# Step sizes as sixteen output rows, B.C as two half-array products, and a new order of the queues in a two-direction state-space kernel

## The chip, the core and the metric

The kernel runs on one core of a Trainium2 chip. The time is the device time of one execution in microseconds (us); lower is better. A core has engines that each work through their own queue in order: TensorE (PE) for matmuls, VectorE (DVE), ScalarE (ACT), GpSimd (POOL), and SyncE (SP), which here only issues transfers (DMAs). TensorE writes its results to PSUM[...]; everything else lies in SBUF, with 128 partitions (rows). An engine waits for another where it needs that one's result, or where a buffer that it is to fill is still being read.

## What is computed

For 8 sequences of 512 tokens with 256 features, a layer norm is followed by two state-space blocks (one forward in time, one on the reversed sequence), whose outputs are projected, joined and added to the input; then a second layer norm and a linear map with a low-rank part are added.

```python
def _mamba2(x, Win, convw, convb, dtb, Alog, Dsk, normw, Wout):
    zxbcdt = x @ Win
    z, xBC, dt = jnp.split(zxbcdt, [D_INNER, D_INNER + CONV_CH], axis=-1)
    xBC = jax.lax.conv_general_dilated(xBC, convw, window_strides=(1,), padding=[(D_CONV - 1, 0)], dimension_numbers=('NLC', 'LIO', 'NLC'), feature_group_count=CONV_CH) + convb
    xBC = _silu(xBC)
    xs, Bm, Cm = jnp.split(xBC, [D_INNER, D_INNER + NGROUPS * D_STATE], axis=-1)
    dt = jax.nn.softplus(dt + dtb)
    A = -jnp.exp(Alog)
    dA = jnp.exp(dt * A)

    def step(h, inp):
        dA_t, dt_t, B_t, C_t, x_t = inp
        dBx = jnp.einsum('bh,bn,bhp->bhpn', dt_t, B_t, x_t)
        h = dA_t[:, :, None, None] * h + dBx
        y = jnp.einsum('bn,bhpn->bhp', C_t, h)
        return (h, y)
...
    y = jnp.transpose(ys, (1, 0, 2, 3)) + Dsk[None, None, :, None] * xs
    y = y.reshape(b, l, D_INNER)
    y = y * _silu(z)
    y = y * jax.lax.rsqrt(jnp.mean(y * y, axis=-1, keepdims=True) + 1e-05) * normw
    return y @ Wout
```

There are 8 heads of 64 values, the state has 64 rows, and the convolution has 4 taps per channel. The step sizes `dt` are eight numbers for each token and direction. They decide how fast the state decays, so they are needed before anything else of a chunk can be worked out.

## The kernel before

**Tiling.** A sequence is cut into 4 chunks of 128 tokens. A chunk is computed in closed form: decays between each two tokens of the chunk (`lam`) times the products of C and B between them (`cb`), times x; and the state `h` that comes in from the chunk before. The unit of work is a `Pair` (sequence b, chunk c): the forward direction on chunk c and the backward one on chunk 3 - c. The main loop (L817) makes one pass, a *round*, for each of the 32 pairs. In round i the pair `p` is finished, the next one, `q`, is prepared, blocks of a later sequence are projected and convolved (`work`, from the table `todo`, L792), and the `Tail` of an older chunk (output projection, residual, second norm, last linear map) is carried on. Sequences are taken two by two for the step sizes (`Steps`).

**The order is written by hand.** `pin()` (L60) makes each engine run its instructions in the order in which the program text issues them. So moving a line in the loop moves every instruction that it issues within its engine's queue.

**The parts that matter here, with their lines:**
- `steps_v` (L267): projects the step sizes of two sequences. The weights `wdt` (L103) are 8 columns in a field of zeros; a shifted window of 128 columns puts the 8 heads of each chunk, sequence and direction at their own 8 rows of one 128 x 128 result `pdt`. That takes 16 matmuls (an fp32 matmul makes two records in the profile). ScalarE then computes v, |v| and exp(-|v|) (L281 to L283); `ratio` and `series` (L296, L304) finish softplus on VectorE.
- `Block` (L366): `project` (L372, PE, `pp`), `tap` (L389, ACT), `convolve` (L392, three VectorE operations that read `pp` from PSUM), `silu` (L412). The block `NBLK` holds B and C of one direction; its `silu` writes three tiles of 64 rows each: `bb`, `cbd` (C set into a tile that is zero elsewhere, so that one matmul gives both directions side by side) and `cc`.
- `Pair`: `fetch` (L456, transfers of the decay factors into `lam`), `scan` (L483, DVE), `turn` (L492, PE transposes and ACT copies to `xs`), `scale_x` (L500, POOL), `cb` (L511, PE), `mix` (L519, DVE: lam times cb), `skip` (L524, ACT), `gate` (L532, PE) and `gate_silu` (L544, ACT), `scale_c` (L476, POOL, tile `dec`), `decay_state` (L549, POOL), `outputs` (L557, PE, `py`), `add_state` (L577: a PE product `pst`, then an ACT copy in chunk 0 or a DVE add), `evict` (L591, DVE), `times_gate` (L595, POOL), `square` (L599), `norm_sum`, `norm_mean`, `norm_power` (L602 to L611), `presum` (L616, POOL).
- `Tail`: `bias1` (L632, POOL), `project` (L635, PE, `pm`), `residual` (L645, DVE, with the statistics of the second norm), `scales` (L652, POOL), `norm2` (L655, ACT), `bias2` (L667, POOL), `turn` (L670), `ffn` (L677, `pf`), `add_ffn` (L682, DVE), `store` (L685).
- `turn1` (L251): transposes of a later sequence's normed input (`pxh`), in chunks 1 and 3 of even sequences. `prepare_wf` (L207): weights of the last map, once, in round 2.
- PSUM: one bank for the seed, three for `p_proj`, two for `p_tr` (small products and transposes, `cb` among them) and two for `p_y`. The banks of a pool are handed out in turn, and a new tile waits until its bank's last reader is done.

Of the kernel before, what the change touches and what calls it, by code (L numbers as in the profile page):

```python
# [8 lines left out]
F32 = mybir.dt.float32  # L9
AF = mybir.ActivationFunctionType  # L10
ALU = mybir.AluOpType
# [3 lines left out]
P = 128  # L15
NB, L, DM = 8, 512, 256
# [15 lines left out]
def tile_bimamba_ffn(  # L32
# [55 lines left out]
    def ps(p, shape, name):  # L88
        return p.tile(shape, F32, name=name, tag=p.name)
# [23 lines left out]
    def load_win(d, cols):  # L113
        sp.dma_start(out=win_sb[:, d, :, cols], in_=win[d].rearrange("(k p) n -> p k n", p=P)[:, :, cols])
# [8 lines left out]
    for d in range(2):  # L123
        act.dma_start(
            out=wdt[:, :, 56 + 64 * d:64 + 64 * d],
            in_=win[d].rearrange("(k p) n -> p k n", p=P)[:, :, DT0:DT0 + NH],
        )
        rows = slice(d * 64, (d + 1) * 64)
        for to, j in ((dtb_col, 0), (a_col, 1)):
            act.dma_start(  # L130
                out=to[rows, :], in_=heads[j, d].unsqueeze(0).unsqueeze(2).to_broadcast([NC * NSG, NH, 1])
            )
    for d in range(2):
        load_win(d, slice(0, XBC0))
    for d in range(2):
        sp.dma_start(out=normw_sb[:, d], in_=normw[d].rearrange("(k p) -> p k", p=P))
        for two in range(2):
            sp.dma_start(
                out=dcol[two * HD:(two + 1) * HD, d, :],
                in_=heads[2, d].rearrange("(k two) -> two k", two=2)[two:two + 1, :].to_broadcast([HD, NBLK]),  # L140
            )
# [22 lines left out]
    pool.memset(samed[64:, 64:], 1.0)  # L164
    fold = const.tile([P, 64], F32, name="fold")
    pool.tensor_tensor(fold, ident[:, :64], ident[:, 64:], ALU.add)

    cbd = []
    for i in range(2):
        cbd.append(const.tile([P, NC, 2, P], F32, name=f"cbd{i}"))  # L170
        pool.memset(cbd[i], 0.0)

    wy = const.tile([P, 2, NBLK, DM], F32, name="wy")
    wf = const.tile([P, NK, DM], F32, name="wf")
# [87 lines left out]
    def sm(name, b0, shape=(P, P), bufs=1):  # L262
        return small.tile(list(shape), F32, name=f"{name}_{b0}", tag=name, bufs=bufs)

    F, W = slice(0, 64), slice(64, P)

    def steps_v(b0):  # L267

        pd = ps(p_tr, [P, P], f"pdt_{b0}")
        n = 0  # L270
        for i in range(NSG):
            for c in range(NC):
                w0 = 56 - (c * NSG + i) * NH
                for k in range(NK):
                    pe.matmul(  # L275
                        pd, lhsT=wdt[:, k, w0:w0 + P], rhs=seq[b0 + i]["xhT"][:, k, c * P:(c + 1) * P],
                        start=(n == 0), stop=(n == NSG * NC * NK - 1),
                    )
                    n += 1
        v, e = sm("v", b0), sm("e", b0)  # L280
        act.activation(v, pd, AF.Identity, bias=dtb_col[:, 0:1])  # L281
        act.activation(e, v, AF.Abs)
        act.activation(e, e, AF.Exp, scale=-1.0)  # L283
        return v, e

    class Steps:

# [78 lines left out]
    class Block:  # L366
# [45 lines left out]
        def silu(self):  # L412
            b, d, s = self.b, self.d, self.s
            if self.blk < NBLK:
                act.activation(self.acc, self.acc, AF.Silu)  # L415
                return
            if "bb" not in s:
                s["bb"] = seqp.tile([P, NC, P], F32, name=f"bb_{b}", tag="bb")
                s["cc"] = seqp.tile([P, NC, P], F32, name=f"cc_{b}", tag="cc")
            bs, cs = slice(0, NS), slice(NS, P)  # L420
            for to, rows in ((s["bb"], bs), (cbd[b % 2][:, :, d, :], cs), (s["cc"], cs)):
                half = to[d * NS:(d + 1) * NS]
                act.activation(
                    half if d == 0 else half[:, ::-1, :],
                    self.acc[rows, :].rearrange("p (c t) -> p c t", c=NC), AF.Silu,
                )
# [12 lines left out]
    class Pair:  # L439
# [70 lines left out]

        def cb(m):  # L511

            m.pcb = ps(p_tr, [P, 2, P], f"cb_{m.name}")
            pe.matmul(
                m.pcb.rearrange("p d t -> p (d t)"), lhsT=m.s["bb"][:, m.c, :],
                rhs=cbd[m.b % 2][:, m.c].rearrange("p d t -> p (d t)"), start=True, stop=True,
            )

        def mix(m, d):  # L519
            dve.tensor_tensor(  # L520
                m.lam[d], m.lam[d], m.pcb[:, d, :].unsqueeze(1).to_broadcast([P, NH, P]), ALU.mult
            )

        def skip(m, d):  # L524
# [52 lines left out]
        def add_state(m):  # L577
            if m.c == NC - 1:
                return
            pst = ps(p_proj, [P, DI], f"pst_{m.name}")  # L580
            for d in range(2):
                rows = slice(d * NS, (d + 1) * NS)
                pe.matmul(pst[rows, :], lhsT=m.s["bn"][:, m.c, rows], rhs=m.xw[d], start=True, stop=True)  # L583
            if m.c == 0:
                m.h_new = m.tile("h", (P, DI))
                act.copy(m.h_new, pst)
            else:
                dve.tensor_tensor(m.h_new, m.h_new, pst, ALU.add)
            m.s["h"] = m.h_new

        def evict(m, d):  # L591
# [221 lines left out]
    def begun(at):  # L813
        return [tails[j] for j in range(n) if begin[j] == at]

    st = late = before = None
    for i in range(n):  # L817
        p, q = pairs[i], pairs.get(i + 1)
        b, c = order[i]
# [9 lines left out]
                pairs[i + 2].fetch()  # L829
        if (c == 0 if even else c == 1) and b + 3 < NB:  # L830
            load(b + 3)
        when(t0, "scales", "norm2", "bias2")
        p.decay_state()
        p.outputs()
        for d in range(2):
# [1 line left out]
            p.times_gate(d)  # L837
        p.add_state()
        when(before, "norm_sum", "norm_mean")
        if q:  # L840
            for d in range(2):
                q.turn(d)
        when(work[0], "project", "tap")
        when(t0, "turn")
        for d in range(2):
# [4 lines left out]
        if st and not even and c == 2:  # L850
            st.exponential()
        if q:
            q.cb()
            q.gate(0)
            q.gate_silu(0)
            for d in range(2):
                q.scale_x(d)
            q.scan(0)
        if q:
            q.scan(1)  # L860
# [7 lines left out]
        if st and not even and c == 2:  # L868
# [2 lines left out]
            pairs[i + 2] = Pair(*order[i + 2])  # L871
            pairs[i + 2].fetch()
        when(t0, "ffn", "add_ffn")
        when(before, "norm_power")
        if q:
            q.scale_c()
        when(t, "bias1")
        p.presum()
        if st and not even and c == 2:
            st.weigh()  # L880
# [12 lines left out]
        when(work[1], "project", "tap")  # L893
        if i < 2:
            prepare_wy(i, range(2, NBLK))
        if q:
            q.skip(1)
        when(work[1], "convolve")
        if i == 2:
            prepare_wf()  # L900
        if i == 0:
            steps_last(0)
            steps_total(0)
        if not even and c == 3 and ahead < NB:
            steps_total(ahead)
        if st and not even and c == 1:
            st.ratio()
            st.series()
        if q:
# [2 lines left out]
        if even and c in (1, 3) and ahead < NB:  # L912
            turn1(ahead + (c == 3), 0)
            turn1(ahead + (c == 3), 1)
        if c == 2 and b + 1 < NB:
            tokenwise_b(b + 1)
        when(work[1], "silu")
# [74 lines left out]
```

## Time and profile before

| | |
|---|---|
| Three runs | 665.66 us median, 665.1 to 667.6 |
| The profiled execution | 668.52 us, span from first to last instruction 666.5 us |
| Mean granted TensorE clock | 0.983 of full speed |
| Step-size projection `pdt`, L275 | 128 records in four calls, 15.0 us busy |
| B.C `cb`, L514 | 64 records, 20.1 us busy |
| `cbd` activations, L423 | 16, 10.1 us busy |
| First bias add, L633, and second, L668 (POOL) | 32 each, 23.3 us busy each |
| Table loads of ScalarE | 12 in the loop, 1.28 us each, and those of the start |

The profiled execution took 2.0 us more than its span, and 2.9 us more than the median of the three runs. Busy time of a group is time in which at least one of its instructions ran. A line of the timeline has start and length in us, engine, line, operation, output and inputs, shapes, and in brackets the idle time of the engine before it with the instruction that ended it. TensorE is busy for 94% of the span; but a share of busy time is an average over stretches that are limited by different engines, and matmuls are pipelined, so that the lines of the rounds have to be read one by one.

### The profile page before, as it was taken

How to read it: one execution, taken by the hardware profiler on the slowest of the kernel's cores; microseconds unless marked ns; L12 is line 12 of the kernel's file. 1: busy time of each engine (PE TensorE's matmuls, PEld its weight loads, DVE VectorE, ACT ScalarE, POOL GpSimd, SP SyncE). 2: the span in 40 equal slices, each digit the busy share in tenths (PEclk: the TensorE clock that was granted, in tenths of full speed). 3: DMA queues.
4: the chain of work that ended last, by engine and by line, in shares of the span. 5: the costliest groups of instructions: out<-in, count | busy, mean ns of one | idle time of the engine just before them, and what ended most of it. 6: DMA issues, size and time to landing. Idle time of an engine off the chain costs nothing.

```text
span 666.5 us, 12446 instructions
## 1 busy us (share of the span) xinstructions
PE 623.3 (94%) x4652; PEld 478.5 (72%) x4652; DVE 542.0 (81%) x827; ACT 399.8 (60%) x855; POOL 467.2 (70%) x572
## 2 busy tenths in 40 slices
PE   4968998999999999999999999999999998999996
PEld 2556676777776777877777677777877777787785
DVE  4788888788988899977988998877998887886643
ACT  2787565876566565875476574686576654564421
POOL 4447455677854888757856789638876679599983
PEclk9979998999999999999999998999999998999998
DMA  7555332313055312134045322332005432333010
GB/s 207 161 168 143 111 104 49 86 42 102 18 182 142 112 62 90 59 92 143 17 135 147 92 64 80 112 112 103 25 13 179 104 111 80 111 112 111 17 49 32
DMA packets 34940, 64.63 MB, mean 97 GB/s; under 512 B 7680, under 2 KB 22080, under 8 KB 34880
## 3 DMA queue, kind: packets, MB, share of 16 engines
q1 hardware_dynamic: 32736, 63.79, 31.8%
q8 instruction: 37, 0.61, 0.4%
q10 hardware_dynamic: 2144, 0.04, 0.2%
q14 instruction: 23, 0.19, 0.1%
HBM read 59.10 MB, written 4.72 MB: 96 GB/s over the span
## 4 chain that ended last, share of the span: by engine, by line
PE 51%; DVE 24%; POOL 13%; ACT 7%; issue 4%; DVEq 0%; POOLq 0%; ACTq 0%
PE pm L640 11%; PE pp L379 9%; PE pz L538 9%; PE py L563 9%; DVE xc L397 7%; DVE lam L490 4%; PE pf L680 3%; POOL yg L597 3%; DVE lam L520 3%; PE pxs L496 3%; POOL xdt L507 2%; PE pdt L275 2%; DVE x L647 2%; ACT xc L390 2%; PE pst L583 2%
## 5 line engine op out<-in xcount | busy, mean ns | idle before, releaser
L397 DVE SCALAR_TENSOR_TENSOR xc<-pp,conv_sb,xc 128x511 f32<-128x511 f32 x183 | 136.0, 744 | 46.3 <-ACT xc L390 41.9
L379 PE MATMUL pp<-xhT,win_sb 128*128 128x512 f32 x320 | 151.2, 600 | 0.5 <-ACT xhT L710 0.5
L490 DVE TENSOR_TENSOR_SCAN lam<-lam,seed 128x512 f32<-128x512 f32 x128 | 145.6, 1200 | 0.0
L538 PEld LDWEIGHTS pz<-xhT,win_sb 128*128 128x128 f32 x1024 | 125.7, 194 | 10.3 <-issue 7.7
L538 PE MATMUL pz<-xhT,win_sb 128*128 128x128 f32 x1024 | 126.6, 277 | 0.0
L640 PE MATMUL pm<-wy,yg 128*128 128x256 f32 x512 | 115.5, 379 | 0.0
L640 PEld LDWEIGHTS pm<-wy,yg 128*128 128x128 f32 x512 | 97.1, 190 | 13.1
L379 PEld LDWEIGHTS pp<-xhT,win_sb 128*128 128x128 f32 x320 | 57.8, 194 | 45.7 <-issue 42.6
L528 ACT ACTIVATE yg<-xc,dcol 128x128 f32<-128x128 f32 x256 | 80.9, 393 | 0.0
L390 ACT ACTIVATE xc<-pp,conv_sb 128x512 f32<-128x512 f32 x64 | 49.3, 774 | 44.9 <-PE pp L379 44.7
L520 DVE TENSOR_TENSOR lam<-lam,cb 128x1024 f32<-128x1024 f32 x64 | 75.0, 1212 | 0.1
L668 POOL TENSOR_TENSOR x<-x,bf_sb 128x256 f32<-128x256 f32 x32 | 23.3, 729 | 73.6 <-ACT xh L657 71.5
L507 POOL TENSOR_TENSOR xdt<-xs,dw 128x512 f32<-128x512 f32 x64 | 66.5, 1046 | 6.6 <-ACT xs L498 6.6
L563 PE MATMUL py<-lam,xdt 128*64 128x128 f32 x1024 | 66.3, 285 | 0.0
L415 ACT ACTIVATE xc<-xc 128x512 f32<-128x512 f32 x64 | 39.5, 628 | 43.7 <-DVE xc L397 43.4
L563 PEld LDWEIGHTS py<-lam,xdt 128*64 128x64 f32 x1024 | 58.6, 143 | 7.5 <-issue 4.6
L593 DVE TENSOR_TENSOR yg<-py,yg 128x512 f32<-128x512 f32 x64 | 42.2, 685 | 18.0 <-PE py L563 15.5
L507 POOL TENSOR_TENSOR xs<-xs,dw 128x512 f32<-128x512 f32 x48 | 50.1, 1045 | 3.8
L647 DVE SCALAR_TENSOR_TENSOR x<-pm,rms,x 128x256 f32<-128x256 f32 x64 | 30.9, 483 | 25.4 <-POOL x L633 16.5
L496 PE MATMUL pxs<-ident,xc 128*128 128x128 f32 x256 | 39.7, 286 | 12.5 <-ACT rms L609 5.1
L498 ACT COPY xs<-pxs 128x512 f32<-128x512 f32 x64 | 36.1, 586 | 15.4 <-PE pxs L496 15.2
L496 PEld LDWEIGHTS pxs<-ident,xc 128*128 128x128 f32 x256 | 29.8, 151 | 19.2 <-ACT rms L609 6.8
(445 smaller groups left out, 996.0 us busy)
## 6 DMA issues: line engine op xcount, KB each, us to landing
lam<-dat SPq DMA_DIRECT2D x64, 512.0 KB, 5.2
x<-in_x_dram SPq DMA_DIRECT2D x36, 128.0 KB, 2.2
out_dram<-x SPq DMA_DIRECT2D x32, 128.0 KB, 1.7
x<-in_x_dram SPq DMA_DIRECT2D x7, 512.0 KB, 6.8
win_sb<-in_win_dram SPq DMA_DIRECT2D x2, 640.0 KB, 5.8
win_sb<-in_win_dram SPq DMA_DIRECT2D x2, 512.0 KB, 7.9
wot<-in_wout_t_dram SPq DMA_DIRECT2D x2, 512.0 KB, 12.4
wo_sb<-in_wo_dram SPq DMA_DIRECT2D x2, 256.0 KB, 8.9
```

The source lines that it names most:

```text
L379: pe.matmul(pp, lhsT=win_sb[:, d, k, c0:c0 + P], rhs=s["xhT"][:, k, :], start=(k == 0), stop=(k == NK - 1),)
L390: act.activation(self.acc, self.pp, AF.Identity, bias=self.w[:, 4:5], scale=self.w[:, 3:4])
L397: dve.scalar_tensor_tensor(self.acc[:, to], self.pp[:, of], self.w[:, 3 - j:4 - j], self.acc[:, to], ALU.mult, ALU.add,)
L490: dve.tensor_tensor_scan(lam, lam, sd, 0.0, ALU.mult, ALU.add)
L496: pe.transpose(pt[:, blk * P:(blk + 1) * P], m.s["xc", d][:, blk, m.tcol[d]], ident)
L507: pool.tensor_tensor(hb(to), hb(m.xw[d]), dw[:, j, cols].unsqueeze(2).to_broadcast([P, NH, HD]), ALU.mult)
L520: dve.tensor_tensor(m.lam[d], m.lam[d], m.pcb[:, d, :].unsqueeze(1).to_broadcast([P, NH, P]), ALU.mult)
L528: act.activation(yg[:, blk, :], m.s["xc", d][:, blk, m.tcol[d]], AF.Copy, scale=dcol[:, d, blk:blk + 1])
L538: pe.matmul(pz[:, blk, :], lhsT=win_sb[:, d, k, blk * P:(blk + 1) * P], rhs=m.s["xhT"][:, k, m.tcol[d]], start=(k == 0), stop=(k == NK - 1),)
L563: pe.matmul(m.py[d][two * HD:(two + 1) * HD, blk, :], lhsT=lhsT, rhs=rhs, start=first, stop=last, skip_group_check=True,)
L640: pe.matmul(t.pm[:, d, :], lhsT=yg[:, blk, :], rhs=wy[:, d, blk, :], start=(blk == 0), stop=(blk == NBLK - 1),)
L647: dve.scalar_tensor_tensor(t.x1[:, 0, :], t.pm[:, d, :], t.s["rs", d, t.c], t.x1[:, 0, :], ALU.mult, ALU.add)
```

## The change

For sequences 2 to 7 (two at a time, three calls), `steps_raw` replaces `steps_v`: the weights `wd2` hold the 16 columns of both directions; each sequence's 512 tokens stream once for each half of the features, and the 16 rows of result for the first sequence go to rows 0 to 15, those of the second to rows 64 to 79 of one PSUM tile. ScalarE copies them out, and 16 small transfers move each group of 8 rows x 128 tokens to the rows at which `Steps` wants them. The softplus operations of ScalarE move from the end of chunk 3 of an even sequence to chunk 1 of the following one. Sequences 0 and 1 still use `steps_v`.

B.C becomes two matmuls, one per direction, that contract 64 rows each (rows 0 to 63 and 64 to 127) and write two PSUM tiles; `cbd` and its activation go. The rest are moves in the loop.

```diff
+    wd2 = const.tile([P, NK, 2 * NH], F32, name="wd2")
     for d in range(2):
         load_win(d, slice(0, XBC0))
+        sp.dma_start(
+            out=wd2[:, :, d * NH:(d + 1) * NH],
+            in_=win[d].rearrange("(k p) n -> p k n", p=P)[:, :, DT0:DT0 + NH],
+        )
...
-    cbd = []
-    for i in range(2):
-        cbd.append(const.tile([P, NC, 2, P], F32, name=f"cbd{i}"))
-        pool.memset(cbd[i], 0.0)
...
+    def softplus_v(b0, of):
+        v, e = sm("v", b0), sm("e", b0)
+        act.activation(v, of, AF.Identity, bias=dtb_col[:, 0:1])
+        act.activation(e, v, AF.Abs)
+        act.activation(e, e, AF.Exp, scale=-1.0)
+        return v, e
+
+    def steps_raw(b0):
+
+        pd = ps(p_tr, [P, L], f"pdt_{b0}")
+        for k in range(NK):
+            for i in range(NSG):
+                pe.matmul(
+                    pd[64 * i:64 * i + 2 * NH, :], lhsT=wd2[:, k, :], rhs=seq[b0 + i]["xhT"][:, k, :],
+                    start=(k == 0), stop=(k == NK - 1), skip_group_check=True,
+                )
+        raw = convp.tile([P, L], F32, name=f"raw_{b0}", tag="raw", bufs=1)
+        for i in range(NSG):
+            rows = slice(64 * i, 64 * i + 2 * NH)
+            act.copy(raw[rows, :], pd[rows, :])
+        rows = sm("rows", b0)
+        for d in range(2):
+            for c in range(NC):
+                for i in range(NSG):
+                    r = d * 64 + (c * NSG + i) * NH
+                    sp.dma_start(
+                        out=rows[r:r + NH, :], in_=raw[64 * i + d * NH:64 * i + (d + 1) * NH, c * P:(c + 1) * P]
+                    )
+        return rows
...
-            for to, rows in ((s["bb"], bs), (cbd[b % 2][:, :, d, :], cs), (s["cc"], cs)):
+            for to, rows in ((s["bb"], bs), (s["cc"], cs)):
...
-            m.pcb = ps(p_tr, [P, 2, P], f"cb_{m.name}")
-            pe.matmul(
-                m.pcb.rearrange("p d t -> p (d t)"), lhsT=m.s["bb"][:, m.c, :],
-                rhs=cbd[m.b % 2][:, m.c].rearrange("p d t -> p (d t)"), start=True, stop=True,
-            )
+            m.pcb = [ps(p_tr, [P, P], f"cb_{m.name}_{d}") for d in range(2)]
+            for d in range(2):
+                rows = slice(d * NS, (d + 1) * NS)
+                pe.matmul(
+                    m.pcb[d], lhsT=m.s["bb"][rows, m.c, :], rhs=m.s["cc"][rows, m.c, :], start=True, stop=True
+                )
...
-        when(t0, "scales", "norm2", "bias2")
+        when(t0, "scales")
+        if work[0] is None:
+            when(t0, "norm2", "bias2")
         p.decay_state()
         p.outputs()
...
         p.add_state()
         when(before, "norm_sum", "norm_mean")
+        p.new_state()
         if q:
             for d in range(2):
                 q.turn(d)
+        if work[0] is not None:
+            when(t0, "norm2")
         when(work[0], "project", "tap")
...
         if q:
+            q.gate(0)
             q.cb()
-            q.gate(0)
             q.gate_silu(0)
             for d in range(2):
                 q.scale_x(d)
+        if work[0] is not None:
+            when(t0, "bias2")
+        if q:
             q.scan(0)
...
         when(t0, "ffn", "add_ffn")
+        when(t, "bias1")
         when(before, "norm_power")
         if q:
             q.scale_c()
-        when(t, "bias1")
         p.presum()
...
-        if q:
-            q.skip(1)
+        elif i == 2:
+            prepare_wf()
         when(work[1], "convolve")
-        if i == 2:
-            prepare_wf()
...
-        if st and not even and c == 1:
+        if raw is not None and c == 1:
+            st = Steps(b + 1, *softplus_v(b + 1, raw))
+            raw = None
             st.ratio()
             st.series()
...
+        if q:
+            q.skip(1)
         if c == 2 and b + 1 < NB:
             tokenwise_b(b + 1)
...
         if even and c == 3 and ahead < NB:
-            st = Steps(ahead, *steps_v(ahead))
+            raw = steps_raw(ahead)
```

`new_state` is the second half of the old `add_state` (the copy or the add that makes the new `h`), now behind `norm_sum` and `norm_mean`. `norm2` and `bias2` keep their old place only in the last five rounds, in which no later sequence is projected (`work[0]` is None).

More of the change, by code (lines that the diff above doesn't have):

```diff
@@ L279, in steps_v @@
                     n += 1
[L280 to L284, printed above, removed]
+        return softplus_v(b0, pd)
     class Steps:
@@ L511, in cb @@
         def cb(m):
-            m.pcb = ps(p_tr, [P, 2, P], f"cb_{m.name}")
-            pe.matmul(
-                m.pcb.rearrange("p d t -> p (d t)"), lhsT=m.s["bb"][:, m.c, :],
-                rhs=cbd[m.b % 2][:, m.c].rearrange("p d t -> p (d t)"), start=True, stop=True,
-            )
+            m.pcb = [ps(p_tr, [P, P], f"cb_{m.name}_{d}") for d in range(2)]
[4 more added lines that the diff above has]
+                )
         def mix(m, d):
             dve.tensor_tensor(
-                m.lam[d], m.lam[d], m.pcb[:, d, :].unsqueeze(1).to_broadcast([P, NH, P]), ALU.mult
+                m.lam[d], m.lam[d], m.pcb[d].unsqueeze(1).to_broadcast([P, NH, P]), ALU.mult
             )
@@ L579, in add_state @@
                 return
-            pst = ps(p_proj, [P, DI], f"pst_{m.name}")
+            pst = m.pst = ps(p_proj, [P, DI], f"pst_{m.name}")
             for d in range(2):
@@ L583, in add_state, with new_state @@
                 pe.matmul(pst[rows, :], lhsT=m.s["bn"][:, m.c, rows], rhs=m.xw[d], start=True, stop=True)
+        def new_state(m):
+            if m.c == NC - 1:
+                return
             if m.c == 0:
                 m.h_new = m.tile("h", (P, DI))
-                act.copy(m.h_new, pst)
+                act.copy(m.h_new, m.pst)
             else:
-                dve.tensor_tensor(m.h_new, m.h_new, pst, ALU.add)
+                dve.tensor_tensor(m.h_new, m.h_new, m.pst, ALU.add)
             m.s["h"] = m.h_new
@@ L814, in begun @@
         return [tails[j] for j in range(n) if begin[j] == at]
-    st = late = before = None
+    st = raw = late = before = None
     for i in range(n):
```

## The prediction

> **What bounds the kernel now.** I read the busy line of the page first, then the busy time round by round, then the table of waits, then the timeline of the rounds in which a wait ends last. A "round" is one pass of the main loop (one chunk of one sequence); I number them 0 to 31 and take the first state product `py` (L563) as a round's start.
>
> ```profile
> PE 623.3 (94%) x4652; PEld 478.5 (72%) x4652; DVE 542.0 (81%) x827; ACT 399.8 (60%) x855; POOL 467.2 (70%) x572
> ```
>
> TensorE (PE) looks like the bound. Rounds 10 to 15 say more (eight rounds, two sequences, make one period of the same work) (columns: stretch, length, then PE, PEld, DVE, ACT, POOL busy, clock, DMA share, GB/s):
>
> ```profile
> 246.00:266.10 20.10, 19.72 (x152) 14.66 (x151) 17.72 (x32) 9.82 (x22) 16.14 (x20) 1.00 0.33 117
> 266.10:288.70 22.60, 22.60 (x185) 18.56 (x184) 17.83 (x25) 17.05 (x35) 13.30 (x20) 1.00 0.40 117
> 288.70:306.70 18.00, 18.00 (x117) 13.32 (x116) 15.30 (x21) 13.20 (x27) 14.12 (x16) 1.00 0.26 77
> 306.70:322.30 15.60, 15.60 (x141) 12.82 (x140) 13.88 (x19) 9.21 (x21) 12.66 (x12) 1.00 0.22 69
> 322.30:343.50 21.20, 20.35 (x157) 15.07 (x157) 20.31 (x42) 13.14 (x27) 15.96 (x21) 1.00 0.07 20
> 343.50:362.90 19.40, 18.59 (x147) 14.16 (x146) 17.59 (x27) 12.58 (x29) 12.54 (x18) 1.00 0.60 189
> ```
>
> Rounds 11 to 13 leave TensorE no gap; in round 14 VectorE (DVE) is busy 20.31 of 21.20 us and TensorE waits for it. So the bound changes hands: TensorE to about 307 us, VectorE after it. The waits say what holds VectorE up:
>
> ```profile
> DVE xc L397 <- ACT xc L390: 41.9, 24, 3.0
> DVE x L647 <- POOL x L633: 16.5, 10, 3.9
> ```
>
> The first is largely a loop of its own: VectorE ends one convolution, ScalarE (ACT) does that block's silu and only then the next block's first tap (0.63 + 0.76 us), and VectorE waits 1.43 us. No faster TensorE shortens that. The second is the bias add L633, queued on GpSimd (POOL) behind `dec` (L479). The turn of rounds 11 and 12 shows both kinds:
>
> ```profile
> 285.07 3.73 PE L275 MATMUL pdt<-xhT,wdt 128*128 128x128 f32 x32
> 285.55 0.63 ACT L423 ACTIVATE cbd<-acc 64x512 f32<-64x512 f32 x1
> 287.53 2.32 DVE L397 SCALAR_TENSOR_TENSOR xc<-pp,conv_sb,xc 128x511 f32<-128x511 f32 x3 [3.00 <-ACT xc L390]
> ...
> 302.91 1.00 DVE L647 SCALAR_TENSOR_TENSOR x<-pm,rms,x 128x256 f32<-128x256 f32 x2 [2.21 <-POOL x L633]
> 303.34 0.78 ACT L390 ACTIVATE xc<-pp,conv_sb 128x512 f32<-128x512 f32 x1 [2.26 <-PE pp L379]
> 304.51 2.28 DVE L397 SCALAR_TENSOR_TENSOR xc<-pp,conv_sb,xc 128x511 f32<-128x511 f32 x3
> ```
>
> And round 13 shows what a matmul costs, by the distance from one group's start to the next:
>
> ```profile
> 306.74 1.10 PE L563 MATMUL py<-dec__2751,h__2819 64*64 64x128 f32 x32
> 307.77 1.97 PE L563 MATMUL py<-lam,xdt 128*64 128x128 f32 x32
> 309.57 1.03 PE L583 MATMUL pst<-xs,bn 128*64 128x512 f32 x4
> 310.52 0.61 PE L605 MATMUL ss<-ones,sz__2645 128*128 128x1 f32 x4
> 313.91 0.60 PE L514 MATMUL cb<-cbd,bb 128*128 128x256 f32 x2
> 314.35 1.95 PE L538 MATMUL pz<-xhT,win_sb 128*128 128x128 f32 x16
> ```
>
> A record (half of an fp32 matmul) of 256 columns takes (314.35-313.91)/2 = 0.22 us, so 128 columns take 0.11 and 512 take 0.43. `pst` has four of 512 in 0.95 us, not 1.7: its two column groups overlap. The 32 records of the first `py` line take 1.03 us, not 3.5: four tiles overlap. Overlapped streaming alone would be 32/4 x 0.11 = 0.88 there and 0.86 for `pst`; the rest, 0.09 to 0.15 us, is paid where the shape of the tiles changes.
>
> [...]
>
> **The change part by part.**
>
> *Step sizes.* `steps_v` took 3.67 us of TensorE (285.07 to 288.74). `steps_raw` has 4 matmuls, 8 records of 512 columns in two column groups: 4 x 0.43 = 1.72 us[...]: 1.9. Saved: 1.75 us, three times (rounds 3, 11, 19). Two ScalarE copies (0.59 each, from L498) replace the three activations and a table load there (2.3 us); those move to chunk 1 of the next sequence, where they run while VectorE still has mixing and residual to do: exp ends some 1.5 us before `ratio` wants it; uncovered, that would be 2.3 us. SyncE issues 16 small transfers more (0.44 us each, as one of the pair `lam<-dat` that takes 0.88: 7 us), queued before the next `lam` and `dec` fetches. Those were issued at 281.69 and 282.66 and slip to about 296; `lam` lands 5.2 us later (page, median), and its scan starts at 312.25. Two rounds lie between the transfers and `ratio`, so I cost them at nothing. The two transfers of `wd2` at the start go before weights that are first used some 30 us later.
>
> *B.C in row groups.* Stream: 4 records of 128 overlapping in twos, 0.22 us[...]: 0.40 to 0.52, where it took 0.44. I take +0.06 a round, +0.2 by the tap of round 12; ends -0.2 (changes free) and +0.3. So this part gains nothing on TensorE. It takes away an activation of 0.63 us (`cbd`) per block. At the end of an even sequence's chunk 3 the moved `skip(1)` (4 x 0.3 us) stands before the same activations and eats that; at the end of an odd one nothing does. Two PSUM buffers are now held until both `mix` are through; the transpose `pxh`, which already waited 1.11 us for the last `mix`, waits for the same end. B.C itself now waits for the copies of both transposes before it, with `pf` and `pm` queued behind; in round 12 those copies end at 295.91 (xT, L675), and the new place, behind a gate projection of 1.78 us, is 296.7.
>
> *The bias adds, `norm2`, `new_state`, `prepare_wf`.* GpSimd adds the first bias ahead of `dec` (2.36 us earlier), so the 16.5 us of waits shrink to those for `norm_power`. `norm2` behind the copies of x is covered by the projection (1.72 us against 1.7 for copies and norm). `dec` ends up to 1.4 us later; in rounds 10 and 18 it is then just in time for `py`.
>
> **The sum for a period.** Rounds 11 to 13: VectorE could come 2.2 us sooner (wait of 302.91), but the convolution of 304.51 needs a tap that TensorE releases: 1.75 - 0.2 sooner, plus the 0.39 us that the tap was early (304.12 to 304.51): 1.9. Rounds 13 to 18 are VectorE and its ScalarE loop; there 0.6 (`cbd` at 364.72) and 0.7 (the bias wait at 380.18) go. Together 3.2 us.
>
> Rounds 2 to 9: TensorE waits 2.41 us before the `py` at 110.95 for `wf`, which VectorE now does 2.2 us sooner. VectorE gains only 0.3 by this (the 1.43 us loop stands free again), then about 1.1 at round 3's end (0.5 before the convolution of 127.64, the rest at 132.86), 2.2 at the bias wait of 146.35, 0.6 and 0.7 as above: 4.9. Rounds 10 to 17 and 18 to 25: 3.2 each. Prologue 0.6 (one `cbd` on the chain at 36.46; the zeroing of `cbd` at 3.1 us is covered, ScalarE's table load ends only at 8.71). Round 0: 0.6. From round 27 GpSimd is busy without a stop but for 0.7 us a round, and its work is the same: 0.8 for rounds 26 to 31. Sum: 0.6 + 0.6 + 4.9 + 3.2 + 3.2 + 0.8 = 13.3 us. The profiled execution took 668.52 us (span 666.5 and 2.0 around it), which gives 655.2; it was 2.9 above the median of the runs shown, so for the median 652.4: I say 652.
>
> **The rivals.**
> 1. *The 16-wide column groups don't overlap* (the part does not do what it says). Then `steps_raw` is 8 x 0.43 = 3.4[...], as before, and round 12 gains 0.2 in place of 1.9: two periods of 1.5, sum 9.9, 656. For it: no 16-wide tile is in the trace. Against: `pst` overlaps at 64.
> 2. *VectorE's waits all go* and TensorE never holds it: 2.2 + 0.6 + 0.6 + 0.7 + 1.0 (the wait of 1.16 for `h` in round 10) = 5.1 a period, and the half-speed `py` stretches at 401 and 555 us (3.2 us together) don't return: sum 0.6 + 0.6 + 4.9 + 10.2 + 3.2 + 0.8 = 20.3, 645. Against: the tap of 303.34 waits for TensorE.
> 3. *Slower[...].* In place of 0.44 us it would take 0.43 of serial stream[...]: 1.3, or 0.9 x 32 = 28.8 us more on TensorE. Less the 13.3, and some 5 that TensorE's present gaps take up: about 676. It decides from 0.85 us per B.C on (13.3/32 more). For it: no 64-row, 128-column tile is in the trace.[...]
> 4. *No change*: `skip(1)`, the later `dec` and the held PSUM buffers together give back some 0.36 us a round (11.5 in all): 664. For it: `skip(1)` eats one `cbd` already; against: the others have the slack named above.
>
> **How the numbers follow.** Chances: my forecast 0.52, rival 1 0.17, rival 2 0.11, rival 3 0.13, rival 4 0.07. My forecast's own range is 647 to 658 (B.C's two ends, +-0.3 x 16 rounds in which TensorE leads, about 5). With rivals 1, 2 and part of 4 the range is 642 to 663. About 0.5% (3.3 us) is what can be told from no change. Faster by more: 0.52 + 0.17 + 0.11 = 0.80; within: 0.07; slower: 0.13.
>
> **What would show it.** Right: `pd` at about 1.9 us; B.C at 0.4 to 0.5; residual L647's wait for GpSimd near 2 or 3 us in all; convolution waits of 2.72 near 2.1 and of 3.00 hardly less; `py` of round 3 without its 2.41. Wrong: B.C over 0.8; a new wait of `evict` for `skip(1)`, or of `ratio` for the exp; `py` waiting for `dec`; TensorE without gaps in rounds 14 to 16.

## The result, and the profile after

The changed kernel takes 655.27 us (median of 4 runs, 654.47 to 656.33); beside it the kernel before took 665.38 (662.96 to 667.6). The ratio is 0.9852, with a 95% interval of 0.9823 to 0.9881: 10.1 us less. The profiled executions are further apart, 668.52 before and 655.07 after; point 1 on the prediction says what is known of that.

In the changed kernel the state product `py` is at L591, the gate projection `pz` at L566, B.C at L543, the step sizes at L280, the convolution at L424 and its first tap at L417, the residual at L679, the two bias adds at L665 and L700, `dec` at L506. First the busy line of the page of the changed kernel:

```profile
PE 616.7 (94%) x4644; PEld 464.5 (71%) x4644; DVE 541.6 (83%) x827; ACT 393.8 (60%) x845; POOL 463.8 (71%) x570
```

TensorE is busy for 6.6 us less, and its share of the shorter span is the same 94%. The stretches of rounds 10 to 15 (same columns as before, cut at the starts of `py`):

```profile
240.40:260.10 19.70, 19.69 (x157) 14.65 (x157) 17.52 (x31) 10.33 (x26) 17.00 (x23) 1.00 0.41 134
260.10:281.11 21.01, 21.01 (x163) 15.12 (x162) 16.29 (x22) 15.59 (x34) 12.59 (x18) 1.00 0.13 39
281.11:299.29 18.18, 18.18 (x120) 13.31 (x118) 16.37 (x22) 11.02 (x25) 14.01 (x16) 1.00 0.29 86
299.29:315.07 15.78, 15.78 (x144) 12.82 (x143) 14.20 (x19) 10.90 (x23) 12.30 (x13) 1.00 0.58 161
315.07:335.90 20.83, 20.07 (x157) 14.87 (x156) 20.01 (x40) 14.67 (x32) 16.04 (x21) 1.00 0.07 19
335.90:355.74 19.84, 18.80 (x149) 14.18 (x148) 17.92 (x28) 12.10 (x29) 12.71 (x18) 1.00 0.61 187
```

Rounds 10 to 13 now have no gap on TensorE at all, so their lengths are simply the sum of what TensorE does. Round 11 lost 1.56 us (22.62 before, 21.06 now). Rounds 12 and 13 became longer by 0.18 each, which is the new B.C; in round 11, 1.75 us saved on the step sizes less the same 0.18 make the 1.56. Rounds 14 and 15 are still VectorE's; round 15 grew by 0.4. Two waits of the changed kernel answer to the two shown of before:

```profile
DVE xc L424 <- ACT xc L417: 45.6, 27, 3.5
DVE x L679 <- POOL x L665: 1.9, 1, 1.9
```

The bias wait fell from 16.5 to 1.9 us; one other wait of the residual for GpSimd, 3.0 us in round 31, is new. The convolution's wait rose from 41.9 to 45.6. The turn of rounds 11 and 12 shows where it rose (timeline of the changed kernel; VectorE, ScalarE and TensorE):

```profile
281.65 2.31 DVE L424 SCALAR_TENSOR_TENSOR xc<-pp,conv_sb,xc 128x511 f32<-128x511 f32 x3 [3.50 <-ACT xc L417]
...
278.23 1.29 ACT L556 ACTIVATE yg<-xc,dcol 128x128 f32<-128x128 f32 x4
279.55 0.63 ACT L450 ACTIVATE bb<-acc 64x512 f32<-64x512 f32 x1
...
279.29 1.90 PE L280 MATMUL pdt<-xhT,wd 128*16 128x512 f32 x8
```

The moved `skip(1)` (L556) stands in ScalarE's queue ahead of the silus of B and C and of the next tap, and VectorE waits 3.50 us where it waited 3.00. TensorE is not held up by this: `py` follows the step sizes at 281.11 without a gap. And B.C with its neighbours in round 11:

```profile
266.38 1.95 PE L566 MATMUL pz<-xhT,win_sb 128*128 128x128 f32 x16
268.26 0.49 PE L543 MATMUL cb<-cc,bb 64*128 64x128 f32 x4
268.68 1.13 PE L712 MATMUL pf<-wf,xT 128*128 128x256 f32 x4
269.64 3.62 PE L672 MATMUL pm<-wy,yg 128*128 128x256 f32 x16
```

From one group's start to the next: `pz` 1.88, B.C 0.42, `pf` 0.96; the records of B.C's two halves start in pairs, 0.007 us apart, so the halves overlap. Before, `pz` took 1.78 (from 314.35, in the lines of the prediction) and `pf` 0.86:

```profile
316.13 1.03 PE L680 MATMUL pf<-wf,xT 128*128 128x256 f32 x4
317.00 3.62 PE L640 MATMUL pm<-wy,yg 128*128 128x256 f32 x16
```

So B.C costs 0.42 itself and 0.1 in each neighbour: 0.62 where it cost 0.44. That is the 0.18 of rounds 12 and 13.

### The profile page after: what moved, and what is told of

Its sections match the earlier page's. It is cut to its first block, busy times and chain, and to the rows that moved or that the text cites. A ratio compares the mean times of both kernels' runs of the same rounds, so it can differ in the third digit from the quotient of the medians.

```text
span 653.3 us, 12516 instructions
## 1 busy us (share of the span) xinstructions
PE 616.7 (94%) x4644; PEld 464.5 (71%) x4644; DVE 541.6 (83%) x827; ACT 393.8 (60%) x845; POOL 463.8 (71%) x570
## 4 chain that ended last, share of the span: by engine, by line
PE 50%; DVE 27%; POOL 9%; ACT 8%; issue 4%; DMA 1%; ACTq 0%; POOLq 0%; DVEq 0%
PE pp L406 11%; PE pm L672 11%; PE pz L566 10%; DVE xc L424 8%; DVE lam L517 6%; PE py L591 6%; PE pf L712 4%; DVE lam L548 3%; PE pxs L523 2%; ACT xc L417 2%; DVE yg L625 2%; PE pst L611 1%; POOL xdt L534 1%; ACT xc L442 1%; POOL yg L629 1%
## 5 line engine op out<-in xcount | busy, mean ns | idle before, releaser
L424 DVE SCALAR_TENSOR_TENSOR xc<-pp,conv_sb,xc 128x511 f32<-128x511 f32 x183 | 136.2, 745 | 50.0 <-ACT xc L417 45.6
L566 PEld LDWEIGHTS pz<-xhT,win_sb 128*128 128x128 f32 x1024 | 123.4, 194 | 10.7 <-issue 9.4
L566 PE MATMUL pz<-xhT,win_sb 128*128 128x128 f32 x1024 | 126.7, 277 | 0.0
L672 PEld LDWEIGHTS pm<-wy,yg 128*128 128x128 f32 x512 | 97.1, 190 | 13.2
L556 ACT ACTIVATE yg<-xc,dcol 128x128 f32<-128x128 f32 x256 | 81.3, 393 | 0.0
L417 ACT ACTIVATE xc<-pp,conv_sb 128x512 f32<-128x512 f32 x64 | 49.2, 773 | 38.7 <-PE pp L406 38.5
L591 PE MATMUL py<-lam,xdt 128*64 128x128 f32 x1024 | 64.5, 280 | 0.0
L591 PEld LDWEIGHTS py<-lam,xdt 128*64 128x64 f32 x1024 | 56.6, 139 | 9.2 <-issue 6.7
L641 ACT ACTIVATE rms<-ss,eps_col 128x2 f32<-128x2 f32 x32 | 8.4, 262 | 55.1 <-PE ss L637 55.1
L679 DVE SCALAR_TENSOR_TENSOR x<-pm,rms,x 128x256 f32<-128x256 f32 x64 | 30.8, 481 | 11.5 <-PE pm L672 4.8
```

Source lines behind the costliest of these rows:

```text
L417: act.activation(self.acc, self.pp, AF.Identity, bias=self.w[:, 4:5], scale=self.w[:, 3:4])
L424: dve.scalar_tensor_tensor(self.acc[:, to], self.pp[:, of], self.w[:, 3 - j:4 - j], self.acc[:, to], ALU.mult, ALU.add,)
L556: act.activation(yg[:, blk, :], m.s["xc", d][:, blk, m.tcol[d]], AF.Copy, scale=dcol[:, d, blk:blk + 1])
L566: pe.matmul(pz[:, blk, :], lhsT=win_sb[:, d, k, blk * P:(blk + 1) * P], rhs=m.s["xhT"][:, k, m.tcol[d]], start=(k == 0), stop=(k == NK - 1),)
L591: pe.matmul(m.py[d][two * HD:(two + 1) * HD, blk, :], lhsT=lhsT, rhs=rhs, start=first, stop=last, skip_group_check=True,)
L672: pe.matmul(t.pm[:, d, :], lhsT=yg[:, blk, :], rhs=wy[:, d, blk, :], start=(blk == 0), stop=(blk == NBLK - 1),)
```

## Experiments

Diffs are against the changed kernel, and so are differences of time where nothing else is said. The runs were made in three groups. The kernel before, timed beside each, took 665.77 us beside the runs with the step sizes back, all moves back, the moves alone and skip(1) back; 666.57 beside the last four; and 665.64 beside the others (665.38 beside the changed kernel itself). So a difference of about 1 us between runs of different groups says nothing.

**Step sizes back.**

```
-            raw = steps_raw(ahead)
+            st = Steps(ahead, *steps_v(ahead))
...
-        if raw is not None and c == 1:
-            st = Steps(b + 1, *softplus_v(b + 1, raw))
-            raw = None
+        if st and not even and c == 1:
```

> The changed kernel with the old step sizes alone put back (128 columns wide, summed in one PSUM tile; the activations of the softplus at the end of chunk 3 again). Theory 1 (the prediction's sum): TensorE sets the pace of rounds 11 to 13 and 19 to 21, so the 1.75 us saved on it come through, less 0 to 0.3; with some 0 to 1 us in the first period the kernel takes 3 to 5 us more than the changed one's 655.3, about 659. Theory 2 (VectorE and its loop with ScalarE hold the period, a faster TensorE only makes TensorE wait): within 1 us of 655.3, and the wait of the first tap for TensorE in rounds 12 and 20 takes up what is lost.

659.88 us (659.32 to 661.67): 4.6 more than the changed kernel, as theory 1 has it. In the profiles rounds 3, 11 and 19 take 23.49, 22.80 and 22.80 us in place of 21.74, 21.06 and 21.06, and the other rounds of the period hardly differ: 1.75 us three times, just what TensorE saves.

**All moves back** (the bias adds, `norm2`, the new state, `wf`, `skip(1)`, the gate projection).

> The changed kernel with every move undone (bias adds, norm2, the new state, wf, skip(1), gate ahead of B.C), with the new step sizes and the new B.C kept. Theory 1 (the prediction's sum): the waits for the bias add come back, 2.2 us in each of three periods, and wf's 0.5; 655.3 + 7 = 662. Theory 2 (the moves only shift waits, since dec comes later and skip(1) delays the silu and tap behind it): 654 to 657.

668.77 us (667.82 to 670.23); ratio to before 1.0044, 1.0032 to 1.0055. Neither theory: new step sizes and new B.C together, in the old order, are slower than the kernel before. With the moves undone TensorE waits 11.4 us in all, 23 times, before the second half of B.C for the copy of `xT`, and round 12 takes 19.16 us in place of 18.18. This gave the theory for the next runs.

**The moves alone** (old step sizes and the old B.C with `cbd`; the lines of the diff in the section on the change, taken back).

> The moves alone: the changed kernel with both the old step sizes and the old B.C (with cbd and its third activation). Theory 1 (the prediction's sum): it loses 3 to 5 us for the step sizes and 0.6 us in each of three periods for cbd: about 661. Theory 2 (the new B.C costs TensorE 0.15 to 0.2 us a round through two changes of tile shape, which the trace of the changed kernel suggests, 3 us over the rounds in which TensorE leads, and cbd was hidden): below the run with the old step sizes alone, by 1 to 3 us.

660.74 us (659.22 to 664.33). Against the run with only the step sizes back, 659.88, this is 0.9 more, and the runs overlap: the new B.C neither gains nor loses anything that these runs can tell. (Theory 1 named 661; theory 2 wanted 1 to 3 us less than 659.88.) Rounds 4 and 5, which TensorE fills, say the same from both sides: 17.99 and 15.64 us with the old B.C, 18.18 and 15.78 with the new one, so TensorE pays about 0.14 to 0.19 a round. That the `cbd` activation it saves is worth about as much elsewhere is inferred from the equal times; no run takes it away alone. Against the kernel before (665.77) the moves with the old B.C gain 5.0 us; which of them do was not tried with the old B.C.

**skip(1) back.**

```
+        if q:
+            q.skip(1)
         when(work[1], "convolve")
...
-        if q:
-            q.skip(1)
         if c == 2 and b + 1 < NB:
```

> The changed kernel with skip(1) put back ahead of the second convolution, all else kept. Theory 1 (the prediction): behind turn1 or ahead of the convolution, skip(1) is covered but for the 0.6 us it eats at the end of an even sequence: 654 to 655.5. Theory 2 (in its new place skip(1) stands in ScalarE's queue between a convolution and its silu, and the next tap and convolution wait for it: waits of 3.5, 1.7 and 1.63 us in rounds 11, 10 and 12 of the changed kernel, where 3.0, 1.43 and 1.43 stood): 0.5 + 0.3 + 0.2 us a period or more come back, 652 to 654. Theory 3 (evict needs skip early, or the tap needs ScalarE free of it): slower, 656 to 658.

653.90 us (653.77 to 655.49), 1.4 less, with overlapping runs. The longest wait for the tap falls from 3.5 to 2.5 us, as theory 2 has it, but round 11 takes 21.06 us as in the changed kernel: TensorE fills it. The spans of the two profiled executions, 653.5 and 653.3, show no gain. Not decided; at most a small loss by the move.

**B.C ahead of the gate projection.**

```
-            q.gate(0)
             q.cb()
+            q.gate(0)
```

> The changed kernel with B.C put back ahead of the gate projection, all else kept. Theory 1 (the gate's place is what makes the new B.C cheap: with the moves undone, the second half of B.C waited 0.50 us for the copy xT, since its PSUM buffer was still held, and B.C took 1.40 us from start to end in place of 0.42): about 1.0 us more in every round in which TensorE leads, some 4.5 us a period and 12 to 14 in all, so 667 to 669. Theory 2 (the loss without the moves came from the bias adds and skip(1)): 655 to 658.

668.36 us (667.26 to 669.97): 13.1 more, by one line, as theory 1 has it. The timeline of this run, round 11:

```profile
270.53 0.38 PE L705 MATMUL pxt<-ident,xh 128*128 128x128 f32 x2
270.84 0.49 PE L543 MATMUL cb<-cc,bb 64*128 64x128 f32 x2
271.83 0.48 PE L543 MATMUL cb<-cc,bb 64*128 64x128 f32 x2 [0.50 <-ACT xT L707]
272.24 2.05 PE L566 MATMUL pz<-xhT,win_sb 128*128 128x128 f32 x16
```

The two halves no longer start together. The first gets its PSUM tile at once; the second waits for ScalarE's copy of `pxt` to `xT`. Its inputs have nothing to do with `xT`, and `pxt` and the tiles of B.C come from the same two banks in turn, so the buffer that it takes is still held by `pxt`. TensorE stands idle for 0.50 us, and the two halves stream one after the other: 1.40 us from start to end in place of 0.42. Behind the gate projection, 1.9 us later, the copy is done: in the changed kernel it ended at 267.40, and B.C began at 268.26.

**The gate's place alone** (all other moves undone, new step sizes and B.C kept).

> New step sizes and new B.C, with every move undone except the gate projection ahead of B.C. Theory 1 (the gate's place carries the moves): 655 to 658. Theory 2 (the prediction's sum: the waits for the bias add are worth 2.2 us in each of three periods, wf 0.5): 661 to 663.

656.06 us (655.55 to 656.98), as theory 1 has it. With the new B.C, of all the moves this one carries nearly everything: 12.7 us against the run with no move, and the changed kernel with all of them is only 0.8 below.

**First bias add back behind dec.**

```
         when(t0, "ffn", "add_ffn")
-        when(t, "bias1")
         when(before, "norm_power")
         if q:
             q.scale_c()
+        when(t, "bias1")
```

> The changed kernel with the first bias add put back behind dec, all else kept. Theory 1 (the prediction): the waits of the residual for GpSimd come back, 2.2 us in each period, of which TensorE or a later convolution wait takes up half or less: 658 to 662. Theory 2 (where TensorE leads, VectorE's earlier residual only lengthens its next wait): 655 to 656.5; and the ends of the last rounds gain up to 1 us, since dec comes sooner there.

671.83 us (670.73 to 675.00): 16.6 more, a miss for both theories. The timeline of this run at the turn of rounds 9 and 10 (GpSimd, VectorE, TensorE):

```profile
244.30 2.38 POOL L506 TENSOR_TENSOR dec__2184<-dec__2184,cc 128x1024 f32<-128x1024 f32 x1
246.63 0.73 POOL L665 TENSOR_TENSOR x<-x,bo_sb 128x256 f32<-128x256 f32 x1
...
247.40 1.00 DVE L679 SCALAR_TENSOR_TENSOR x<-pm,rms,x 128x256 f32<-128x256 f32 x2 [0.87 <-POOL x L665]
...
248.46 1.97 PE L591 MATMUL py<-dec__2184,h__2200 64*64 64x128 f32 x28 [1.18 <-DVE x L679]
250.36 3.68 PE L591 MATMUL py<-lam,xdt 128*64 128x128 f32 x32
```

The chain is bias add, residual, release of the PSUM tile `pm`, `py`. Since the second bias add (L700) was moved to stand between the scaling of x and `dec`, everything behind it on GpSimd is 0.7 us later, and with `dec` in front the first bias add is too late for TensorE too. After that gap `py` ran at half speed: 3.68 us in place of 1.97; the granted clock was 0.50 from 247.8 to 254.7. Round 10 took 24.11 us in place of 19.64. This profile is the slowest of the six executions (675.00 us). They were granted a mean clock of 0.976 to 0.985, where the changed kernel's four had 0.986 to 0.988. So a part of the 16.6 us that was not measured apart is the clock.

**norm2 and the second bias add back at the head of the round.**

```
         when(t0, "scales")
-        if work[0] is None:
-            when(t0, "norm2", "bias2")
+        when(t0, "norm2", "bias2")
...
-        if work[0] is not None:
-            when(t0, "norm2")
...
-        if work[0] is not None:
-            when(t0, "bias2")
```

> The changed kernel with norm2 and the second bias add put back to the head of the round, all else kept. Theory 1 (the prediction: covered): within 0.7 us of 655.3. Theory 2 (norm2, which waits for GpSimd's scale and shift, holds ScalarE's queue ahead of the state's copy, rms and the copies of x, and TensorE waits for these): 2 to 4 us more, 657 to 659. Theory 3 (GpSimd's bias add at the head of the round delays the decay of the state): the same sign, with a wait of the product with the state for GpSimd.

653.18 us (652.35 to 653.81): 2.1 less, outside all three theories, so these two moves lose time. The four executions were also granted a little more clock (0.988 to 0.991, against 0.986 to 0.988), but the two profiles show the loss without it: over rounds 2 to 25, in each of which both have a granted clock of 1.00, the changed kernel takes 450.96 us and this one 448.94. The waits of the changed kernel, then those of this run:

```profile
PE pxh L258 <- DVE lam L548: 1.6, 4, 0.5
PE py L591 <- POOL dec__2184 L506: 0.5, 1, 0.5
PE py L591 <- POOL dec__3744 L506: 0.5, 1, 0.5
PE py L591 <- POOL dec__5281 L506: 0.5, 1, 0.5
```

```profile
PE pxh L258 <- DVE lam L548: 0.8, 2, 0.4
POOL x L700 <- ACT xh L689: 60.2, 29, 5.5
```

The three waits of the changed kernel for `dec` stand before the `py` of rounds 10, 18 and 26. With the second bias add back at the head, where GpSimd waits anyway for `xh` (the last line), `dec` begins 0.7 us sooner behind the scaling of x: those three waits are gone and half of `pxh`'s, and rounds 9, 17 and 25 are shorter by 0.94, 0.67 and 0.55 us. That is not all gain: rounds 10, 18 and 26 become 0.55 longer each, and rounds 7, 15 and 23, in which VectorE leads, 0.4 shorter. Which of the two moved lines does it was not tried.

**skip(1) and norm2 both back.**

> The changed kernel with norm2 and the second bias add at the head of the round again and skip(1) ahead of the second convolution again; step sizes, B.C, the gate's place, the first bias add ahead of dec, the new state and wf as changed. Theory 1 (the two moves cost 2.1 and 1.4 us independently, as the two single runs say): 651.5 to 652.5. Theory 2 (they cost the same waits in rounds 0 to 2 and 9, 10, so only one of them comes back): 653 to 654.

652.77 us (651.01 to 653.38), between the theories: no more than `norm2` alone can be told from it.

**The same, with the first bias add behind dec in the last five rounds.**

> The run before with one thing more: in the last five rounds the first bias add stands behind dec. In the changed kernel the state product waited 0.77 and 1.77 us for dec in rounds 28 and 30. Theory 1 (these waits are on the chain that ends last): 1 to 2 us less than the run before, 650 to 651. Theory 2 (GpSimd is full in these rounds, what dec gains the bias add and the residual behind it lose): within 0.7 us of it.

652.40 us (650.53 to 653.33), as theory 2 has it. The wait of 1.8 us for `dec` before `py` in round 30 shrank to 0.2, and in its place `py` waited 1.0 us in round 29 and 1.3 in round 30 for the residual.

**Only two moves: the gate, and the first bias add ahead of dec.**

> New step sizes and B.C, and of the moves only two: the gate ahead of B.C, and the first bias add ahead of dec. Stands against the run with the gate's place alone (656.06). Theory 1 (the prediction: the waits for the bias add are 2.2 us a period, of which something is taken up elsewhere): 2 to 4 us less, 652 to 654. Theory 2 (VectorE's earlier residual only lengthens the wait for the next tap): 655.5 to 656.5.

651.92 us (651.18 to 652.67), ratio to before 0.9779, 0.9758 to 0.9799. It is 4.1 below the run with the gate's place alone, as theory 1 has it (that run belongs to another group). Its waits:

```profile
DVE xc L424 <- ACT xc L417: 38.6, 26, 2.4
DVE x L679 <- POOL rms L644: 1.9, 1, 1.9
```

The bias wait is gone as in the changed kernel, and the convolution waits 7.0 us less than there. The further moves of the change (`norm2`, the second bias add, the new state, `wf`, `skip(1)`) together cost 3.35 us by the medians. The profiles say the same with less: over rounds 4 to 25 the run with the gate's place alone takes 413.15 us, the changed kernel 412.97, the run with `norm2` and the second bias add back 410.94 (these two at a granted clock of 1.00 in each of the rounds), and this one 410.54. So there the first bias add is worth 2.6 us and the further moves cost 2.4, 2.0 of it by `norm2` and the second bias add. This simplest version is the best of all by its median; the two runs before it overlap with it.

**Transfers cut in two** (32 in place of 16).

```
-                    sp.dma_start(
-                        out=rows[r:r + NH, :], in_=raw[64 * i + d * NH:64 * i + (d + 1) * NH, c * P:(c + 1) * P]
-                    )
+                    for t in (slice(0, 64), slice(64, P)):
+                        sp.dma_start(
+                            out=rows[r:r + NH, t],
...
```

> The changed kernel with each of the 16 row transfers cut in two: 32 transfers on SyncE's queue, the same bytes. In the changed kernel the 16 took 11.15 us there, and the fetch of lam behind them went out at 293.35 and its scan began at 304.68; with 5.2 us to landing (of the page of before), some 5 us of cover are left. Theory 1 (the transfers cost nothing only as long as that cover lasts): 11 us later, lam comes 5 to 6 us late in each of three periods; 665 to 672. Theory 2 (the queue issues ahead of need, nothing waits): 655 to 657.

666.86 us (663.76 to 672.00): 11.6 more, as theory 1 has it. The timelines (SyncE's queue and VectorE) of the changed kernel, then of this run:

```profile
282.10 11.15 SPq L293 DMA_DIRECT2D rows<-raw  x16
293.35 0.86 SPq L487 DMA_DIRECT2D lam<-dat  x2
...
304.68 2.33 DVE L517 TENSOR_TENSOR_SCAN lam<-lam,seed 128x512 f32<-128x512 f32 x2
```

```profile
286.29 21.91 SPq L294 DMA_DIRECT2D rows<-raw  x32
308.30 0.97 SPq L489 DMA_DIRECT2D lam<-dat  x2
...
312.26 4.77 DVE L519 TENSOR_TENSOR_SCAN lam<-lam,seed 128x512 f32<-128x512 f32 x4 [3.30 <-DMA lam<-dat]
```

The first has no wait in front of the scan: `lam` goes out 11 us ahead of it. In the second it goes out 4 us ahead, and the scan waits 3.30 us. With the same bytes the queue is held for 21.91 us in place of 11.15, so the cost goes with the number of transfers: 21.91/32 = 0.68 us each here, 11.15/16 = 0.70 in the changed kernel. VectorE passes its delay on. GpSimd's first bias add waits for the `x` that SyncE fetches behind the rows (three times, 4.6 us in all; in the changed kernel never), `dec` stands behind it, and so TensorE waits for `dec` in rounds 6 and 14:

```profile
PE py L593 <- POOL dec__2999 L508: 2.6, 1, 2.6
PE py L593 <- POOL dec__1423 L508: 2.5, 1, 2.5
```

The mean granted clock of the 20 executions was 0.968 to 0.982, where the changed kernel's four had 0.986 to 0.988. So the 11.6 us are the late transfers and a part, not measured apart, that goes with the lower clock.

## Why the prediction was near, point by point

The forecast, faster by a gain of 13.3 us, was right in direction and order of size; it was 3.2 us too large against the measured 10.1. Several of its terms were wrong, and some of the errors cancel. The time alone does not tell the forecast (652) from rival 1 (656): the measured 655.3 lies nearer to the rival. It is the length of `pd` that does (point 3).

1. *The basis.* The sum was set against one profiled execution, and took its two half-speed stretches of `py`, at 401 and 555 us, as lasting (granted clock 0.50 for 3.4 us from 401.71 and from 555.31). In the changed kernel's profile these two are gone: round 18 fell from 21.78 us to 19.64, round 26 from 22.04 to 19.64, where round 10, the same work without a stretch, was 20.16 before. That is 1.62 + 1.88 = 3.5 us. The spans differ by 666.5 - 653.3 = 13.2; less 3.5 this leaves 9.7. But that is no clean account: the profile of before has a third such stretch in its loop (0.50 for 3.4 us from 111.58, round 3), and the changed kernel's has two of its own (0.50 for 3.4 us each, from 74.9, round 1, and from 607.4, round 30). Executions differ in this. Of the 27 of the kernel before beside the first experiments, the five with a mean granted clock of 0.990 took 663.1 to 664.5 us, the two with 0.981 took 668.2 and 668.9, and just over half had 0.986; the profiled one had 0.983. So the agreement of 13.2 with the sum of 13.3 is chance, and the medians are the measure.
2. *Where in the loop.* By the starts of `py`, rounds 2 to 9 gained 4.2 us (4.9 forecast), 10 to 17 2.5 (3.2), 18 to 25 3.8 with 1.6 of the stretch in it, so 2.2 (3.2), 26 to the end 1.35 with 1.9 of the stretch, so -0.5 (0.8). Up to round 2 it was 1.3 (1.2), but the start of round 0 lies anywhere from 49.0 to 51.9 us in four runs with the same code up to there, so that figure says little. From round 2 to 25 each stretch fell short by about the same 0.7 to 1; point 8 has the cause of most of it.
3. *Step sizes: right.* `pd` takes 1.82 us from start to start (1.9 forecast: 1.72 of stream and up to 0.2 that I estimated for the change of tile shape). The records of its two column groups start in pairs, 0.007 us apart, and the next pair 0.42 to 0.43 us later: they overlap, and rival 1 falls. The gain of 1.75 came through in all three places and measured 4.6 us by itself.
4. *The transfers: right in that they cost nothing, wrong in size.* I took 0.44 us each, 7 us; they take 11.15 us on the queue, 0.70 each, and `lam` goes out 12.2 us into round 12, where 7.3 were forecast. The cover is real but thin: twice as many cost 11.6 us.
5. *B.C: the size was off.* I took +0.06 us a round for two changes of tile shape; it is +0.18, the term of the sum that was mis-sized. My estimate for one change was the 0.09 to 0.15 us that `pst` and `py` took beyond their stream, twice that for B.C, but that is one side of it. Both the group before and the group after lengthen by 0.1 (the last record of `pz` stands for 0.21 us in place of 0.11, the first of `pf` for 0.32 in place of 0.22), and within B.C each of the two pairs stands for 0.21 us in place of 0.11. The halves do overlap, and rival 3 falls at 0.62 against its point of 0.85; of its 1.3 us a B.C, 0.9 beyond the stream was an estimate that nothing measured bears out. The forecast gave this part nothing on TensorE and 0.6 us a period for `cbd`; nothing of the whole could be measured.
6. *The gate's place: seen, and not priced.* The prediction says that B.C now waits for the copies of both transposes and that the new place is late enough, which the trace shows. It did not ask what the same B.C costs in the old place. The runs did: 13 us. So a slower outcome was near, though from another cause than rival 3's: a PSUM buffer still held (0.50 us of waiting), and the two halves one after the other (1.40 us in place of 0.42). In the old order the change is 0.44% slower than before, and one exchanged line decides.
7. *The first bias add: right.* The residual's waits for GpSimd shrank from 16.5 to 4.9 us (1.9 and 3.0; 2 to 3 forecast). With the gate's place settled, this is worth 4.1 us by the medians, 2.6 of it in rounds 4 to 25.
8. *norm2 and the second bias add: called covered, they cost 2.1 us.* The step that failed is "`dec` ends up to 1.4 us later; in rounds 10 and 18 it is then just in time for `py`": it is 0.5 us too late there and in round 26, and `pxh` waits 0.8 us more. With these two lines back, rounds 2 to 9 gain 5.4 us on the kernel before (its stretch of half clock in round 3 in them) and rounds 10 to 17 gain 3.0, where 4.9 and 3.2 were forecast: without this step the sum is about right there. A `py` that waits for `dec` was among the prediction's own signs of being wrong. These two moves are also what makes the first bias add so dear in its old place (16.6 us, the clock included, in place of 4.1).
9. *skip(1)*: the eaten `cbd` gain is confirmed (the wait of 3.00 became 3.50), and TensorE covers it. *wf*: the 2.41 us before `py` in round 3 are gone, as said; in the version with two moves they are back as 2.2, without that version being slower.

Rival 2 falls: in round 12 the tap still waits 3.33 us for TensorE. Rival 4 had the right kind of cause, small waits given back, and the wrong size.

## What to carry to other kernels

The two halves of B.C, which overlap, took two PSUM buffers at the same moment. Where one matmul is split like this, look at what holds the next buffer of the pool at that place, and put other TensorE work ahead until its copy is done: it decided the sign here (668.36 us against 655.27). Price a change of tile shape on both sides of it (here 0.2 us on the way in and 0.2 on the way out: 0.62 in all for 0.22 of stream), and a row transfer by its slot in the queue, not by its bytes (here 0.70 us for 4 KB and 0.68 for 2 KB). Try the moves of a change one by one and in small sets: two of them were worth 16.8 us, the others cost 3.4, and the same bias add was worth 4 or 17 us depending on what else stood in GpSimd's queue, with the drop of the granted clock to 0.50 that came with it.

## What was not expected of the hardware

- A transfer of 4 KB between two SBUF tiles holds SyncE's queue for 0.70 us (11.15/16), one of 2 KB for 0.68; a `lam` fetch of 512 KB takes 0.43 (0.86/2).
- In the run with the first bias add back TensorE fell to a granted clock of 0.50 for 6.8 us (from 247.8), with a gap of 1.18 us at the start of it; from 244.0 to 248.4 us TensorE was busy for 2.08 of 4.4 us. In round 18 of the same run TensorE stood idle for 1.17 us and the clock stayed at 1.00. At the clock of 0.50 `py` took 3.68 us in place of 1.97, so these gaps went with a loss of another 1.7 us beyond their own length. What decides whether the clock falls was not shown: no run moved a gap to test it.
